# Two GNN layers on one core: mask loading reordered in the opening, and the search for negative mask values moved to later steps

## The chip, the cores and the metric

The kernel runs on one core of a Trainium2 chip. The metric is device time in microseconds. TensorE (PE in the profile) multiplies matrices into PSUM; VectorE (DVE), ScalarE (ACT) and GpSimd (POOL) work on tiles in SBUF, the first two also on PSUM; SyncE (SP) issues most DMAs. Each engine works through its own queue in program order.

## The reference

The input x is (8, 2048, 256) in float32, adj is a (2048, 2048) int32 mask with 0 and 1. Two layers follow each other, each added to its input:

```python
h = jnp.maximum(_layernorm(x, axis=-1), 0.0)
x = x + _L0_gnn_ref(h, adj, ...)   # 4 heads of 64; softmax inside each chunk of 256 keys
h = jnp.maximum(_layernorm(x, axis=-1), 0.0)
x = x + _L1_gnn_ref(h, adj, W, a)  # e = leaky(e_src + e_dst), masked, softmax over 2048 keys, elu
```

In the first layer the mask enters as

```python
scores = jnp.clip(scores, -10.0, 10.0)
mask = adj_matrix.reshape(N, Nc, CHUNK)[None, None]
scores = jnp.where(mask == 0, jnp.asarray(-10.0, scores.dtype), scores)
attn = jax.nn.softmax(scores, axis=-1)
ctx = jnp.einsum('bhnjc,bhjcd->bhnd', attn, vc)
```

and in the second as `mask = adj > 0`. The two tests agree unless adj holds a negative value. So the kernel looks for negative values, and if there is one (or if one of three other bounds is broken) a slower second version of the second layer runs behind the fast one.

## The kernel before

**Masks.** The mask is used turned over, keys on partitions, as an fp8 tile `limit` of 128 x 4 x 16 x 512: -0.5 where a key is masked, +0.5 where it is not. A score tile is cut with one VectorE instruction, the minimum of the score and its limit (L537). `limits()` makes it from 32 parts of 128 query rows by 1024 keys. For each part: `fetch` (SP loads 512 KB of int32, L262), `turn_over` (ScalarE casts it to bf16, L268, and SP issues a transposing DMA, L272), `find_negative` (ScalarE takes relu(-mask) with a sum over the row into `below`, L283; for the first four parts VectorE takes a minimum, L280 and L281), and `compare` (VectorE writes `limit`, L287). Two raw buffers alternate, so the load of part k + 2 waits for cast and search of part k. One `next` of `mask_turns` does `turn_over`, `find_negative` and the next `fetch`; one of `mask_compares` does one `compare`.

**The order before the loop** is written out by hand: loads of x, Wk, Wq, two biases, two mask parts, the next block of x, Wv, Wo, three bias rows and bv; then the transposes of Wk and Wq; then a string of letters, each one step of a generator: b the first batch's work (normalised rows h, their transposes hT, projections to K and Q), r the statistics of x, m a mask turn, c a compare; then the transposes of Wv and Wo, one compare, two mask turns and one b.

**The main loop** (from `for n in range(-2, len(steps))`) has 256 steps: 8 batches, 4 blocks of 512 queries, 4 chunk pairs by 2 head pairs. Step n makes the scores of step n + 2 (S, 4 tiles of 128 x 1024: TensorE L529, VectorE L537), takes their exponentials (E, ScalarE L543), weighs V with the tiles of step n (C, L551) and adds up the sums of step n + 1 (A, L564). ScalarE copies the sums from PSUM (L575), a DMA regroups them (`sum<-s`), VectorE inverts them (L582), a DMA writes them out (`inv<-sum`) and two read them back spread over the partitions (`r<-inv`), and VectorE scales by them (L603, L605). In mid-step (M, between E2 and C1) and at its end stands `mask_part()`: one compare and one mask turn each, so all 32 parts are done by step 11.

Other work is put between: `tick()` runs the generators in `quiet` (loads, statistics, and the end of a query block, `finish`: where n % 8 is 1 ScalarE makes four rows o from x, L650), and `advance()` those in `aside` (normalised rows L153, transposes L171, projections L162 with PSUM copies L378 for K and Q and L357 for V, the output projection). Scores, projections and sums share three PSUM pairs under the tag "big". The h tiles have a ring of three buffers.

After the loop the second layer runs over 32 passes of 16 key tiles, and the test of `below` comes at the end of it.

Of the kernel before, what the change touches and what calls it, by code (L numbers as in the profile page):

```python
# [10 lines left out]
I32 = mybir.dt.int32  # L11
FP8 = mybir.dt.float8e5
AF = mybir.ActivationFunctionType
ALU = mybir.AluOpType
PSUM = bass.MemoryType.PSUM

P = 128
# [34 lines left out]
def layers(  # L52
# [18 lines left out]
    nc = tc.nc  # L71
# [8 lines left out]
    NT = QB // P  # L80
# [3 lines left out]
    big = ctx.enter_context(tc.tile_pool(name="big", bufs=2))  # L84
    small = ctx.enter_context(tc.tile_pool(name="small", bufs=2))
# [16 lines left out]
    def aux(dtype=F32):  # L102

        return rest[0] if rest else pair(dtype)[:, 0, :]
# [26 lines left out]
    power = const.tile([P, 1], F32, tag="power", name="power")  # L131
# [70 lines left out]
    quiet = []  # L202
# [8 lines left out]
    def tick():  # L211
        moved = False
        for steps_of in list(quiet):
            got = next(steps_of, quiet)
            if got is quiet:
                quiet.remove(steps_of)
            moved = moved or got is not False
        return moved
# [13 lines left out]
    def drain(until=lambda: False):  # L232
        while not until() and advance():
            pass


    limit = const.tile([P, NQB, NKT, QB], FP8, tag="limit", name="limit")
    below = const.tile([P, NQB, 2 * NT], F32, tag="below", name="below")
# [6 lines left out]
    adj_in = [big.tile([P, 1024], I32, tag="kv", name="adj_in", bufs=12) for _ in range(2)]  # L245
    masks = big.tile([P, 2, 1024], BF16, tag="kv", name="masks", bufs=12)
    two_turned = big.tile([P, 2, 8, P], BF16, tag="c1", name="turned", bufs=1)
    turned_masks = [two_turned[:, 0], two_turned[:, 1], big.tile([P, 8, P], BF16, tag="r", name="turned", bufs=1)]
# [5 lines left out]
    def limits():  # L254

        parts = [(qb, t, half) for qb in range(NQB) for half in range(2) for t in range(NT)]

        def fetch(k):
            qb, t, half = parts[k]
            q0 = qb * QB + t * P  # L260
            raw = adj_in[k % 2]
            nc.sync.dma_start(raw, adj[q0 : q0 + P, half * 1024 : (half + 1) * 1024])  # L262
            return raw

        def turn_over(k):

            m = masks[:, k % 2]
            nc.scalar.copy(  # L268
                m.rearrange("p (b t c r) -> p b c t r", b=2, t=NT, c=2),
                raws[k].rearrange("p (b c t r) -> p b c t r", b=2, c=2, t=NT),  # L270
            )
            nc.sync.dma_start(turned_masks[k % 3], m, transpose=True)  # L272

        def find_negative(k):

            qb, t, half = parts[k]
            found = below[:, qb, 2 * t + half : 2 * t + half + 1]
            if k < NT:
                least_of = small.tile([P, 1], I32, tag="bad", name="lowest", bufs=1)
                nc.vector.tensor_reduce(least_of, raws[k], mybir.AxisListType.X, ALU.min)  # L280
                nc.vector.tensor_scalar(found, least_of, 0.0, -1.0, ALU.min, ALU.mult)  # L281
            else:
                nc.scalar.activation(raws[k], raws[k], AF.Relu, scale=-1.0, accum_out=found)  # L283

        def compare(k):
            qb, t, half = parts[k]
            nc.vector.tensor_scalar(  # L287
                limit[:, qb, half * 8 : (half + 1) * 8, t * P : (t + 1) * P],
                turned_masks[k % 3], 0.0, 0.5, ALU.not_equal, ALU.subtract, saturate=False,
            )  # L290
            if t == NT - 1:
                made.append((qb, half))

        raws = [fetch(k) for k in range(2)]

        def turns():
            for k in range(len(parts)):
                turn_over(k)
                find_negative(k)
                if k + 2 < len(parts):  # L300
                    raws.append(fetch(k + 2))
                yield

        def compares():
            for k in range(len(parts)):
                compare(k)
                yield

        return turns(), compares()

    qkv, norm_of = {}, {}

# [143 lines left out]
    first_batch = batch(0)  # L456
    next(first_batch)
    next(quiet[0])
    PART = {"q": 0.5 / EDGE, "k": 1.0}
    wT, raw_of = {}, {}  # L460

    def fetch_weights(name, w, tag):

        raw_of[name] = big.tile([P, FC, F], F32, tag=tag, name="w_raw", bufs=2)
        nc.sync.dma_start(raw_of[name], w.rearrange("(c p) f -> p c f", p=P))

    def turn_weights(name):

        wT[name] = const.tile([P, FC, F], F32, tag=f"w{name}", name=f"w{name}")
        for ic in range(FC):  # L470
            ps = aux()[:, :F]
            for oc in range(FC):
                nc.tensor.transpose(
                    ps[:, oc * P : (oc + 1) * P], raw_of[name][:, oc, ic * P : (ic + 1) * P], ident
                )
            nc.scalar.copy(wT[name][:, ic, :], ps)
# [3 lines left out]
    bcol = {}  # L480
# [2 lines left out]
        nc.sync.dma_start(bcol[name], v.rearrange("(c p) -> p c", p=P))  # L483
    mask_turns, mask_compares = limits()
    next(quiet[0])
    fetch_weights("v", Wv, "o")
    fetch_weights("o", Wo, "o")
    brow = {}
    for name, v in (("o", bo), ("gamma", gamma), ("beta", beta)):
        brow[name] = const.tile([P, F], F32, tag=f"r{name}", name=f"r{name}")  # L490
# [1 line left out]
    bv_col = small.tile([P, 2], F32, tag="bv", name="bv", bufs=1)  # L492
    nc.sync.dma_start(bv_col, bv.rearrange("(s p) -> p s", p=P))

    turn_weights("k")
    turn_weights("q")
    nc.scalar.mul(bcol["q"], bcol["q"], PART["q"])
    for what in "b b m b b m m c b b m c r b b c".split():
        next({"b": first_batch, "r": quiet[0], "m": mask_turns, "c": mask_compares}[what])
    turn_weights("v")  # L500
    turn_weights("o")
    for what in (mask_compares, mask_turns, mask_turns, first_batch):
# [2 lines left out]
    def bias():  # L505
        spread_bv = big.tile([P, 2, P], F32, tag="h", name="spread_bv", bufs=3)
        nc.vector.tensor_copy(spread_bv, bcast(bv_col, 2, P))
        yield from later()
        ps = aux()[:, :F]
        for s in range(2):  # L510
            nc.tensor.matmul(
                ps, spread_bv[:, s, :], wT["o"][:, s, :], start=(s == 0), stop=(s == 1)
            )
        nc.vector.scalar_tensor_tensor(brow["o"], ps, float(NCH), brow["o"], ALU.mult, ALU.add)
        yield
# [376 lines left out]
    def last_batch():  # L892
        yield from batch(B - 1)
        aside.append(sources_of(W, a))
        yield from preparation(0)
# [30 lines left out]
    weights, totals, r = {}, {}, None  # L926
    ORDER = [(kind, int(t)) for kind, t in "S0 E0 S1 E1 C0 S2 E2 M0 C1 S3 E3 C2 C3 B0 A0".split()]
    for n in range(-2, len(steps)):
        here[0] = n
        if n >= 0:  # L930
            b, qb, c = steps[n]
            blk, hp = divmod(c, 2)
            if n == NT:
                aside.append(bias())
            b1 = 1 if n == 1 else b + 2 if (qb, c) == (NQB - 1, NCH - 2) else B
            if b1 < B:
                aside.append(batch(b1) if b1 + 1 < B else last_batch())
            if b == B - 1 and c == NCH - 2 and qb < NQB - 1:
                aside.append(fill(qb))
            drain(lambda: len(qkv[b][2]) > blk)  # L940
            both = banks("both")
            v = qkv[b][2][blk]
        coming = prepared(steps[n + 2]) if n + 2 < len(steps) else iter(())
        inside = -1 <= n < len(steps) - 1
        weights[n + 2] = []
        for kind, t in ORDER:
            if kind in "SE":
                weights[n + 2] += [e for e in (next(coming, None),) if e is not None]
            elif kind == "A":
                if inside:  # L950
                    sums = pair()[:, 0, :256]
                    add_up(totals.pop(n + 1), sums)
                    got = divide(sums)
            elif kind == "B":
                if 0 <= n < 4:
                    advance(False)
            elif kind == "M":
                mask_part()
            elif n >= 0:
                weigh(hp, t, weights[n][t], v, both)  # L960
        weights.pop(n, None)
        if n + 2 < len(steps):
            totals[n + 2] = added(weights[n + 2])
        if n >= 0:
            if c == 0:
                accs[qb] = heads_tile("acc", "acc")
            accumulate(accs[qb][:, hp, :], both, r, blk == 0)
            if c == NCH - 1:
                finish(b, qb, accs[qb])
        held = invert(got) if inside else None  # L970
        if n >= 0:
            tick()
        if inside:
            r = spread(held)
        fetch_all()
        for _ in range({-2: 5, 3: 2}.get(n, 3 if n < NQB * NCH else 2)):
            advance(n < 0)
        mask_part()
# [55 lines left out]
    bad = small.tile([P, 4], F32, tag="bad", name="bad", bufs=1)  # L1034
# [148 lines left out]
    for s, (k, jt) in enumerate(rounds):  # L1183
        here[0] = len(steps) + s // 4
        at[0] = s
        b, h = passes[k]
# [19 lines left out]
        m = jt // 2  # L1206
# [320 lines left out]
```

## Time and profile before

| | us |
|---|---|
| median of 3 runs (lowest to highest) | 3971.54 (3970.2 to 3981.95) |
| profiled execution | 3974.03 |
| its span | 3972.2 |

| stretch, us | PE busy | ACT busy | DVE busy | DMA share | GB/s |
|---|---|---|---|---|---|
| 0 to 210 | 170.96 | 159.47 | 136.70 | 0.75 | 174 |
| 210 to 420 | 202.45 | 121.77 | 168.35 | 0.28 | 75 |
| 300 to 2600 | 2256.16 | 1395.90 | 1923.93 | 0.32 | 85 |

The first 210 us hold all the mask work. Instructions that the change touches: the cast L268 32 x 1.03 us, the search L283 28 x 1.06 us with an accumulator read of 0.19 each, the search L280 4 x 1.22 us, the compare L287 32 x 0.68 us (median), the transposing DMA L272 32 issues of 1.26 us (median) on SP.

In such lines a bracket gives the engine's idle time ahead of the instruction and what ended it; "SPq" is SP issuing a DMA, whose length there is that of the issue, not of the transfer. In the lines of digits each digit is the busy share of a slice in tenths.

### The profile page before, as it was taken

How to read it: one execution, taken by the hardware profiler on the slowest of the kernel's cores; microseconds unless marked ns; L12 is line 12 of the kernel's file. 1: busy time of each engine (PE TensorE's matmuls, PEld its weight loads, DVE VectorE, ACT ScalarE, POOL GpSimd, SP SyncE). 2: the span in 40 equal slices, each digit the busy share in tenths (PEclk: the TensorE clock that was granted, in tenths of full speed). 3: DMA queues.
4: the chain of work that ended last, by engine and by line, in shares of the span. 5: the costliest groups of instructions: out<-in, count | busy, mean ns of one | idle time of the engine just before them, and what ended most of it. 6: DMA issues, size and time to landing. Idle time of an engine off the chain costs nothing.

```text
span 3972.2 us, 93255 instructions
## 1 busy us (share of the span) xinstructions
PE 3846.7 (97%) x38454; PEld 1359.6 (34%) x38454; DVE 3409.6 (86%) x3920; ACT 2527.0 (64%) x3635; POOL 3380.8 (85%) x1763
## 2 busy tenths in 40 slices
PE   7899999999999999999999998989999999999997
PEld 2233333333333333333333333323333333333332
DVE  5778888888888888888888877879999999999998
ACT  7756556666566566656665656556766667676666
POOL 4678899999899899999999988858778778788887
PEclk9999999999999999999999999999999999999999
DMA  7723333333333333333333333322223122232222
GB/s 184 175 74 82 82 82 88 82 83 93 83 82 85 84 84 82 90 84 80 86 90 81 77 91 84 88 75 78 57 66 76 47 74 67 55 72 62 55 55 50
DMA packets 379442, 324.33 MB, mean 82 GB/s; under 512 B 261504, under 2 KB 329856, under 8 KB 379008
## 3 DMA queue, kind: packets, MB, share of 16 engines
q1 hardware_dynamic: 373312, 301.24, 29.8%
q0 software_dynamic: 4608, 16.78, 1.2%
q8 instruction: 304, 4.98, 0.5%
q14 instruction: 130, 1.06, 0.1%
q10 hardware_dynamic: 1088, 0.26, 0.0%
HBM read 271.26 MB, written 36.18 MB: 77 GB/s over the span
## 4 chain that ended last, share of the span: by engine, by line
PE 64%; DMA 13%; DVE 9%; POOL 5%; ACT 4%; issue 3%; SPq 1%; DVEq 0%; POOLq 0%; ACTq 0%
PE acc L1003 17%; PE big L529 15%; PE both L551 13%; PE big L162 7%; PE den L1014 6%; DMA r<-inv 5%; POOL t L1214 3%; DMA sum<-s 3%; DMA inv<-sum 3%; DVE E L537 3%; PE rest L162 2%; PE big L564 2%; DVE e L993 2%; ACT E L543 2%; DMA x<-in_x_dram 2%
## 5 line engine op out<-in xcount | busy, mean ns | idle before, releaser
L543 ACT ACTIVATE E<-E 128x1024 f32<-128x1024 f32 x1024 | 1081.8, 1058 | 683.1 <-DVE E L537 623.8
L537 DVE SCALAR_TENSOR_TENSOR E<-big,limit 128x1024 f32<-128x1024 f32 x1024 | 1198.6, 1214 | 91.5 <-PE big L529 85.9
L923 POOL TENSOR_TENSOR add<-add,E 128x1024 f32<-128x1024 f32 x512 | 1216.3, 2376 | 40.3 <-ACT E L543 0.2
L993 DVE SCALAR_TENSOR_TENSOR e<-near,far,limit 128x2048 f32<-128x2048 f32 x512 | 1166.6, 2341 | 30.7 <-issue 16.1
L529 PE MATMUL big<-qT,kT 64*64 64x512 f32 x8192 | 1069.6, 601 | 34.7 <-DVE E L537 11.8
L551 PE MATMUL both<-E,v 64*64 64x512 f32 x8192 | 1075.1, 592 | 9.4 <-DVE acc L605 6.2
L1214 POOL TENSOR_TENSOR t<-t,e 128x1024 f32<-128x1024 f32 x384 | 911.7, 2420 | 188.3 <-PE den L1014 99.7
L1003 PE MATMUL acc<-e,qn 128*32 128x512 f32 x8192 | 979.1, 595 | 11.8 <-DVE e L993 11.6
L921 POOL TENSOR_TENSOR add<-E 128x1024 f32<-128x1024 f32 x256 | 629.2, 2458 | 209.1 <-ACT E L543 208.7
L1173 ACT ACTIVATE t<-e,quot 128x1024 f32<-128x1024 f32 x384 | 419.8, 1141 | 200.3 <-PE den L1014 148.8
L551 PEld LDWEIGHTS both<-E,v 64*64 64x64 f32 x8192 | 341.8, 134 | 588.0 <-issue 502.1
L529 PEld LDWEIGHTS big<-qT,kT 64*64 64x64 f32 x8192 | 293.6, 133 | 613.0 <-issue 342.8
L1003 PEld LDWEIGHTS acc<-e,qn 128*32 128x32 f32 x8192 | 270.6, 110 | 554.9 <-issue 467.6
L603 DVE TENSOR_TENSOR both<-both,r 128x512 f32<-128x512 f32 x448 | 310.8, 694 | 165.1 <-DMA r<-inv 118.9
L605 DVE TENSOR_TENSOR acc<-both,acc 128x512 f32<-128x512 f32 x448 | 309.8, 692 | 15.3
L1014 PE MATMUL den<-t,for_sums 128*32 128x512 f32 x1536 | 230.6, 593 | 7.7 <-POOL t L1214 7.6
L564 PE MATMUL big<-add,both_of 128*32 128x256 f32 x2048 | 164.0, 392 | 0.0
L1014 PE MATMUL den<-e,for_sums 128*32 128x512 f32 x1024 | 149.9, 592 | 0.0
L582 DVE RECIPROCAL sum<-sum 128x16 f32<-128x16 f32 x256 | 63.7, 249 | 87.8 <-DMA sum<-s 83.8
L162 PE MATMUL big<-hT,wk 128*32 128x512 f32 x1024 | 125.1, 610 | 9.9 <-ACT hT L179 9.9
L1131 ACT ACTIVATE z<-z,dens 128x64 f32<-128x64 f32 x496 | 124.6, 334 | 2.0 <-DVE z L1115 2.0
L162 PE MATMUL big<-wv,hT 128*32 128x256 f32 x2048 | 123.5, 383 | 1.4 <-ACT hT L179 1.3
(142 smaller groups left out, 3060.7 us busy)
## 6 DMA issues: line engine op xcount, KB each, us to landing
r<-inv SPq DMA_DIRECT2D x512, 256.0 KB
x<-in_x_dram SPq DMA_DIRECT2D x96, 512.0 KB
es<-er SPq DMA_DIRECT2D x64, 512.0 KB
adj_in<-in_adj_dram SPq DMA_DIRECT2D x32, 512.0 KB
x<-o POOLq DMA_DIRECT2D x32, 512.0 KB, 4.4
x<-x SPq DMA_DIRECT2D x32, 512.0 KB
xh<-x SPq DMA_DIRECT2D x128, 128.0 KB
out_dram<-xh SPq DMA_DIRECT2D x124, 128.0 KB
```

The costliest lines, as they stand in the source:

```text
L162: nc.tensor.matmul(to[32 * j : 32 * j + 32], lhsT[:, n : n + 32], rhs, start=start, stop=stop)
L529: nc.tensor.matmul(ps[64 * c : 64 * c + 64, hh, :], ks[blk][own, hp, keys : keys + 64], qs[qb][own, hp, :], start=True, stop=True,)
L537: nc.vector.scalar_tensor_tensor(e, ps, -0.5, bcast(limit[:, qb, NT * blk + t, :], 1, 2), ALU.max, ALU.min)
L543: nc.scalar.activation(e, e, AF.Exp, scale=0.25 * EDGE)
L551: nc.tensor.matmul(both[c][64 * hh : 64 * hh + 64, :], v[own, t, mine], e[own, hh, :], start=(t == 0), stop=(t == NT - 1),)
L921: nc.gpsimd.tensor_tensor(total, tiles[0], tiles[1], ALU.add)
L923: nc.gpsimd.tensor_tensor(total, total, e, ALU.add)
L993: nc.vector.scalar_tensor_tensor(e, near, far[:, jt, h : h + 1], limit[:, :, jt, :], ALU.max, ALU.min)
L1003: nc.tensor.matmul(acc[part][32 * blk : 32 * blk + 32, :], qn[jt // NT][:, jt % NT, own], e[:, blk, :], start=(jt == 0), stop=(jt == NKT - 1),
L1014: nc.tensor.matmul(den[32 * blk : 32 * blk + 32, :], for_sums[:, jt, :], blocks[blk], start=first, stop=last,)
L1173: nc.scalar.activation(t, e[:, 2 * half : 2 * half + 2, :], AF.Copy, scale=shared[b][4][:, jt // 2, h : h + 1],)
L1214: nc.gpsimd.tensor_tensor(ts[half], ts[half], now[:, 2 * half : 2 * half + 2, :], ALU.add)
```

## The change

- Four raw parts are loaded at once: parts 2 and 3 into the two buffers of the tag "add", which the loop's sums use later. Parts 4 and 5 are fetched after the casts of parts 0 and 1, so a load follows the cast by four parts there and by two afterwards.
- The casts stand between the steps of the first batch (the new string of letters). The loads of Wv and Wo come after the first two mask turns, the bias rows and bv after the whole string; the transposes of Wk and Wq come first.
- `find_negative` leaves the mask turn. It now reads `limit`, two key tiles by 512 queries at a time (1024 fp8 values a partition), into an fp8 tile of the h ring, and runs on ScalarE once in every step with n % 4 = 1 from 33 to 157, 32 in all, after `tick()` and ahead of the `r<-inv` loads and `advance()`.
- `compare` takes the minimum of the mask and 1, less 0.5, instead of a test against 0, less 0.5. A negative mask value then gives a limit below -0.5.

```diff
--- before.py
+++ after.py
@@ -258,7 +258,7 @@
         def fetch(k):
             qb, t, half = parts[k]
             q0 = qb * QB + t * P
-            raw = adj_in[k % 2]
+            raw = big.tile([P, 1024], I32, tag="add", name="adj_in") if k in (2, 3) else adj_in[k % 2]
             nc.sync.dma_start(raw, adj[q0 : q0 + P, half * 1024 : (half + 1) * 1024])
             return raw
 
@@ -271,34 +271,23 @@
             )
             nc.sync.dma_start(turned_masks[k % 3], m, transpose=True)
 
-        def find_negative(k):
-
-            qb, t, half = parts[k]
-            found = below[:, qb, 2 * t + half : 2 * t + half + 1]
-            if k < NT:
-                least_of = small.tile([P, 1], I32, tag="bad", name="lowest", bufs=1)
-                nc.vector.tensor_reduce(least_of, raws[k], mybir.AxisListType.X, ALU.min)
-                nc.vector.tensor_scalar(found, least_of, 0.0, -1.0, ALU.min, ALU.mult)
-            else:
-                nc.scalar.activation(raws[k], raws[k], AF.Relu, scale=-1.0, accum_out=found)
-
         def compare(k):
             qb, t, half = parts[k]
             nc.vector.tensor_scalar(
                 limit[:, qb, half * 8 : (half + 1) * 8, t * P : (t + 1) * P],
-                turned_masks[k % 3], 0.0, 0.5, ALU.not_equal, ALU.subtract, saturate=False,
+                turned_masks[k % 3], 1.0, 0.5, ALU.min, ALU.subtract, saturate=False,
             )
             if t == NT - 1:
                 made.append((qb, half))
 
-        raws = [fetch(k) for k in range(2)]
+        raws = [fetch(k) for k in range(4)]
 
         def turns():
             for k in range(len(parts)):
                 turn_over(k)
-                find_negative(k)
-                if k + 2 < len(parts):
-                    raws.append(fetch(k + 2))
+                coming = k + 4 if k < 2 else k + 2
+                if k not in (2, 3) and coming < len(parts):
+                    raws.append(fetch(coming))
                 yield
 
         def compares():
@@ -307,6 +296,16 @@
                 yield
 
         return turns(), compares()
+
+    def find_negative(k):
+
+        qb, half, t = k // 8, k % 8 // NT, k % NT
+        room = big.tile([P, 1024], FP8, tag="h", name="room", bufs=3)
+        nc.scalar.activation(
+            room.rearrange("p (k q) -> p k q", k=2),
+            limit[:, qb, 8 * half + 2 * t : 8 * half + 2 * t + 2, :],
+            AF.Relu, scale=-1.0, bias=power[:, 0:1], accum_out=below[:, qb, 2 * t + half : 2 * t + half + 1], saturate=False,
+        )
 
     qkv, norm_of = {}, {}
 
@@ -483,8 +482,17 @@
         nc.sync.dma_start(bcol[name], v.rearrange("(c p) -> p c", p=P))
     mask_turns, mask_compares = limits()
     next(quiet[0])
+    turn_weights("k")
+    turn_weights("q")
+    nc.scalar.mul(bcol["q"], bcol["q"], PART["q"])
+    def begin(letters):
+        for what in letters.split():
+            next({"b": first_batch, "r": quiet[0], "m": mask_turns, "c": mask_compares}[what])
+
+    begin("m b m b b")
     fetch_weights("v", Wv, "o")
     fetch_weights("o", Wo, "o")
+    begin("m b c m b c b r b b c")
     brow = {}
     for name, v in (("o", bo), ("gamma", gamma), ("beta", beta)):
         brow[name] = const.tile([P, F], F32, tag=f"r{name}", name=f"r{name}")
@@ -492,11 +500,6 @@
     bv_col = small.tile([P, 2], F32, tag="bv", name="bv", bufs=1)
     nc.sync.dma_start(bv_col, bv.rearrange("(s p) -> p s", p=P))
 
-    turn_weights("k")
-    turn_weights("q")
-    nc.scalar.mul(bcol["q"], bcol["q"], PART["q"])
-    for what in "b b m b b m m c b b m c r b b c".split():
-        next({"b": first_batch, "r": quiet[0], "m": mask_turns, "c": mask_compares}[what])
     turn_weights("v")
     turn_weights("o")
     for what in (mask_compares, mask_turns, mask_turns, first_batch):
@@ -970,6 +973,8 @@
         held = invert(got) if inside else None
         if n >= 0:
             tick()
+        if n >= 33 and n % 4 == 1 and n // 4 - 8 < 32:
+            find_negative(n // 4 - 8)
         if inside:
             r = spread(held)
         fetch_all()
```

## The prediction

> **What bounds the kernel now.** I read the page first, then the chain of waits, the timeline, and the DMA load in quarter microseconds.
>
> ```profile
> span 3972.2 us, 93255 instructions
> PE 3846.7 (97%) x38454; PEld 1359.6 (34%) x38454; DVE 3409.6 (86%) x3920; ACT 2527.0 (64%) x3635; POOL 3380.8 (85%) x1763
> ...
> PE   7899999999999999999999998989999999999997
> ...
> DMA  7723333333333333333333333322223122232222
> ```
>
> TensorE is full except in the first slices, which are the ones where DMA is full. The stretches say the same: TensorE 171.0 of the first 210 us, 2256 of the 2300 us from 300 to 2600. So there are two places where this change can act: the opening, up to step 11 (about 205 us), where masks are made, and the 32 steps that get the search. Whatever either gives or takes stays to the end, since TensorE has nothing to catch up with.
>
> In the opening the chain of waits puts 28 searches (L283) on the path at about 1.15 us each ("130.35 0.94 issue" and "131.29 0.19 ACT adj_in L283" are the inside of one). The timeline of one step shows what else is there:
>
> ```profile
> 129.26 1.03 ACT L268 CAST masks<-adj_in 128x1024 bf16<-128x1024 int32 x1
> ...
> 130.32 1.23 SPq L272 DMA_TRANSPOSE turned<-masks  x1
> 130.32 1.06 ACT L283 ACTIVATE adj_in<-adj_in 128x1024 int32<-128x1024 int32 x1
> ...
> 131.64 0.53 SPq L262 DMA_DIRECT2D adj_in<-in_adj_dram  x1
> ...
> 132.33 0.35 ACT L575 COPY s<-big 128x256 f32<-128x256 f32 x1
> ...
> 132.71 0.67 SPq L577 DMA_DIRECT2D sum<-s  x1
> ...
> 135.83 0.25 DVE L582 RECIPROCAL sum<-sum 128x16 f32<-128x16 f32 x1 [3.17 <-DMA sum<-s]
> ```
>
> Times are start and length. The cast ends, SP issues the transpose for 1.23 us and at once the next mask part. Beside that, ScalarE searches, does the last exponential and copies the sums. The sums leave at 132.71 and land only 3.1 us later; after step 11, without masks, they need 1.8 to 2.1. The DMA load from 128 us on, a digit per 0.25 us, says why:
>
> ```profile
> DMA  9998799799964189964998869975200000012000
> ```
>
> It is busy until 135.25: the sums land when transpose and mask part have drained.
>
> The later place is a step with n % 8 = 1, here n = 49:
>
> ```profile
> 591.58 0.37 ACT L575 COPY s<-big 128x256 f32<-128x256 f32 x1
> 594.29 2.08 ACT L650 ACTIVATE o<-x,off,rstd 128x256 f32<-128x256 f32 x4 [2.34 <-DMA x<-in_x_dram]
> 596.27 0.67 ACT L378 ACTIVATE qT<-big,bq 128x512 f32<-128x512 f32 x1
> ...
> 596.99 1.09 PE L529 MATMUL big<-qT,kT 64*64 64x512 f32 x8 [1.01 <-ACT qT L378]
> ```
>
> ScalarE waits for x, does four o rows, then empties the PSUM pair of qT; TensorE has already stopped for that pair. Where n % 8 = 5 it is the other way round, ScalarE waits for TensorE:
>
> ```profile
> 477.44 0.69 ACT L378 ACTIVATE kT<-big,bk 128x512 f32<-128x512 f32 x1 [1.05 <-PE big L162]
> ```
>
> **Part one, the loads and the order before the loop.** Parts 2 and 3 go out behind 0 and 1 (two issues of 0.5 us, so x's second block leaves at 5.3 us, not 4.3; its first reader ran at 23.7, so this costs nothing). Wv, Wo, three bias rows and bv (0.51 + 0.68 + 0.92 + 0.34 + 0.43 + 0.38 us of SP's time) go behind the first transposes. Part 0 lands at 9.5 (VectorE's search, L280, waited for it until 9.58). ScalarE now casts it ahead of the first h, which started at 8.98: cast to 10.6, two h to 11.7, cast to 12.7, hT copy to 13.3, two h to 14.4, cast to 15.4, hT copy to 16.0. So K's first matmul moves from 14.79 to 16.05, **1.3 us later**. K and Q took until 24.2 and now take until 25.4; the copies of wv and wo end at 27.4 (26.1). From there it is faster. Parts 4 and 5 are in (issued at about 10.7 and 14 behind the transposes; before, part 5 came at 29.0), and two searches are gone: casts to 29.5, two h to 30.5, then the three E exponentials, which started at 32.2, **1.7 us earlier**. The next cast ends at 34.75 (36.1), then its transpose, mask part 8, and x's last block at 36.7 instead of 38.11. Its landing at 43.14 is what the chain waits for: **-1.4 us**. Bounds: DMA was idle 2.5 us before that landing (29.75 to 31, 36 to 37.25) and the bytes ahead of it are the same, so no more than -2.5; if the late K stays, +1.3. VectorE's four searches (1.22 + 0.15 us each) are hidden by its wait for data; the compare with a minimum costs what the compare with not-equal did, 0.68 us, since only the operation differs.
>
> **Part two, steps -1 to 11, 26 searches gone.** The one at a step's end lies in the wait for the sums: nothing, but for steps 2 and 3 where it delayed an exponential (0.4 by TensorE's idle time there, and 0.3). The one in mid-step delays the last exponential and the sums by 1.06 us (start to next start). But without it the sums cannot leave before SP has issued transpose and part, 1.23 + 0.1 + 0.53 + 0.1 = 1.96 us after the cast; now it is 2.4. That leaves 0.4, and the drain takes most of that: in steps 6, 7 and 8 the sums were there 3.73, 3.79 and 3.83 us after the mask part's issue, whenever they left. Transpose and part themselves leave no sooner. I take nothing for steps 4 to 9, 0.5 and 0.6 for steps 0 and 1, where the sums left late behind an hT copy, and 0.7 for step 10, which fetches no part: **-2.5 us** in all. Bounds: 0, and 13 x 1.06 = -13.8 if the sums followed their own issue.
>
> The Trainium skill (DMA: Bandwidth & Descriptors, section Queues, rings and completion order) says that a DMA's semaphore increment lands only after every earlier write of that DMA engine. By that rule the sums cannot overtake the mask part and steps 4 to 9 give nothing; by a fixed latency from their own issue they would give 0.4 each, 2.4 us more. The load row above agrees with the rule for one step.
>
> **Part three, 32 searches in steps 33 to 157.** The nearest rows are fp8 to fp8 at the same size:
>
> ```profile
> L882 ACT ACTIVATE limit<-limit x32: 1039/1046/1062, 2351.1 to 2640.7; 128x1024 fp8e5<-128x1024 fp8e5 x32
> ```
>
> and L283 with its accumulator read, after which the next instruction starts 1.06 us after the search did. I take 1.06; 1.25 if the read did not overlap. The search follows the o rows and goes ahead of the PSUM copies on ScalarE's queue.
> - 16 steps with n % 8 = 5: ScalarE sat idle 1.05 to 1.4 us before the kT copy. The search fills this: 0 (at most 0.2 each, 3.2).
> - 16 steps with n % 8 = 1: I read, for each, the end of the qT or v copy and the start of the third group of score matmuls. In 12 (41, 49, 57, 65, 97, 105, 113, 121, 129, 137, 145, 153) at most 0.07 us lay between: 12 x 1.01 = 12.1. In 73, 81, 89 it was 0.63, 0.92, 0.66: 0.43 + 0.14 + 0.40 = 1.0. In 33 it was 1.25: 0. Sum **+13.1 us**.
> The queue behind the search holds that copy and the next step's exponentials, which had up to 1.9 us of room; TensorE waits for the copy. From 400 to 1640 us TensorE's listed waits are only 10.4 us, 5.5 of them for just these copies, so little is left to absorb a stall. Lower bound 0, if x landed a microsecond earlier, as it does in step 33; upper 16 x 1.25 + 3.2 = 23. The search's output takes a slot of the h ring (three), whose last readers, the transposes at n % 8 = 3 and 4, are done; limit is written again only from 2351 us. No wait from these.
>
> **Sum.** -1.4 - 2.5 + 13.1 = +9.2 us. The profiled run took 3974.0 (span 3972.2 and 1.8 around it), so 3983.2; it is 2.5 above the median of 3971.5, on which the forecast is **3980.7**, its own range 3975 to 3987.
>
> **Rivals.**
> 1. *The sums follow their own issue*, so every mid-step search was on the path: -13.8 - 1.4 + 13.1 = -2, 3969. For it: the chain of waits counts the search. Against: landing times tied to the part's issue.
> 2. *Faster*: the same, and the later searches fall into ScalarE's idle time (36% over the span), x landing earlier: -15 to -16, 3956. Against: ScalarE is idle there because it waits in order, ahead of the search, not behind it.
> 3. *Slower*: the opening gives nothing, because the cold, late K chain (+1.3) stays ahead of the exponentials, and each late search costs 1.25 at n % 8 = 1 and 0.1 at 5: 1.3 + 15.6 + 1.6 = +18.5, 3990. It decides if K's first matmul comes after 16 us and the first exponential after 32.2.
> 4. *Half the late price*: where x lands varies with DMA traffic that the change shifts; if 6 of the 12 tight steps become like step 33, the late part is 6.6 and the net +2.7: 3974. For it: the copy's room runs from 0 to 1.25 us in the same kind of step.
>
> **Chances.** Forecast 0.53, rival 1 0.10, rival 2 0.13, rival 3 0.15, rival 4 0.09. What a measurement of this kernel can tell from no change is about 0.3%, 11.9 us: below 3959.6 or above 3983.5. The forecast's own range crosses the upper bound: 0.24 of its 0.53 lies above. Faster: 0.13 and a little of rival 1, 0.15. Slower: 0.24 + 0.15 = 0.39. Same: 0.46. The range, 3963 to 3989, leaves out most of rival 2 and half of rival 3.
>
> **What would show it.** Right: the first exponential of E near 30.5 us and x's last block landing near 41.7; in steps 4 to 9 sums that leave 0.4 us earlier and land no earlier; the search between the o rows and the qT or v copy, and TensorE's waits for those copies at n % 8 = 1 grown from 5.5 to about 18 us; nothing at n % 8 = 5. Wrong: steps 5 to 9 shorter by a microsecond each, or no growth of the waits for qT and v.

## The result, and the profile after

Over 18 runs each the changed kernel has a median of 3981.98 us (3973.18 to 3990.58), the kernel before 3973.66 (3963.61 to 3981.95). The ratio is **1.0022**, with a 95% interval of 1.0015 to 1.0029: 8 to 9 us slower, inside the 0.3% taken as no change, but clear of 1. In a later group of runs it was 1.0028 (1.0019 to 1.0038). Forecast: 3980.7, +9.2.

The page of the changed kernel, the lines that answer to those of before:

```profile
span 3982.2 us, 93224 instructions
PE 3842.7 (96%) x38454; PEld 1398.1 (35%) x38454; DVE 3404.5 (85%) x3912; ACT 2530.4 (64%) x3643; POOL 3375.1 (85%) x1763
...
DMA  7722333333333333332332332322223222222222
```

TensorE does the same work in a span 10 us longer. Step 49 of the changed kernel in the timeline (start, length, engine; in brackets the idle time ahead and what ended it):

```profile
592.30 0.37 ACT L578 COPY s<-big 128x256 f32<-128x256 f32 x1
...
594.49 2.07 ACT L653 ACTIVATE o<-x,off,rstd 128x256 f32<-128x256 f32 x4 [1.81 <-DMA x<-in_x_dram]
596.47 1.13 ACT L304 ACTIVATE room<-limit,power 128x1024 fp8e5<-128x1024 fp8e5 x1
597.50 0.18 ACT L304 ACTIVATION_READ_ACCUMULATOR room<-limit,power 128x1 f32 x1
597.60 0.67 ACT L377 ACTIVATE qT<-big,bq 128x512 f32<-128x512 f32 x1
...
598.32 1.09 PE L532 MATMUL big<-qT,kT 64*64 64x512 f32 x8 [1.68 <-ACT qT L377]
```

The search stands between the o rows and the qT copy, and TensorE waits 1.68 us for that copy; before it was 1.01. The list of waits of TensorE from 400 to 1640 us (total, times, longest), first the kernel before, then the changed one:

```profile
PE big L529 <- ACT qT L378: 4.6, 7, 1.0
...
PE big L529 <- ACT v L357: 0.9, 2, 0.5
```

```profile
PE big L532 <- ACT qT L377: 14.8, 11, 2.1
PE big L532 <- ACT v L356: 3.3, 3, 1.9
```

5.5 us have become 18.1. Where n % 8 is 5, here n = 37, the search only fills the wait: the kT copy starts 1.41 us after the copy of the sums (477.64 to 479.05), as it did before (476.03 to 477.44).

```profile
477.64 0.35 ACT L578 COPY s<-big 128x256 f32<-128x256 f32 x1
477.89 1.15 ACT L304 ACTIVATE room<-limit,power 128x1024 fp8e5<-128x1024 fp8e5 x1
...
479.05 0.69 ACT L377 ACTIVATE kT<-big,bk 128x512 f32<-128x512 f32 x1
```

The opening did not go as forecast. ScalarE's timeline there, in the changed kernel:

```profile
12.34 1.09 ACT L153 ACTIVATE h<-x,off,rstd 128x256 f32<-128x256 f32 x2
15.51 1.04 ACT L268 CAST masks<-adj_in 128x1024 bf16<-128x1024 int32 x1 [2.08 <-DMA turned<-masks]
16.46 0.58 ACT L179 COPY hT<-big 128x512 f32<-128x512 f32 x1
17.93 1.04 ACT L268 CAST masks<-adj_in 128x1024 bf16<-128x1024 int32 x1 [0.89 <-DMA turned<-masks]
...
31.36 2.94 ACT L546 ACTIVATE E<-E 128x1024 f32<-128x1024 f32 x3
```

The third cast waits 2.08 us for the transposing DMA of the first part to land, and the fourth 0.89 us for that of the second: the buffer of the cast masks has two halves only, and each is free again once its transpose has read it. K's first matmul comes at 17.09 (before 14.79, forecast 16.05), the first exponential at 31.4 (32.2, forecast 30.5), x's last block lands at 43.95 (43.14, forecast 41.7).

### The profile page after: what moved, and what is told of

The parts are those of the page before. It is cut to its first block, busy times and chain, and to the rows that moved or that the text cites. A ratio compares the mean times of both kernels' runs of the same rounds, so it can differ in the third digit from the quotient of the medians.

```text
span 3982.2 us, 93224 instructions
## 1 busy us (share of the span) xinstructions
PE 3842.7 (96%) x38454; PEld 1398.1 (35%) x38454; DVE 3404.5 (85%) x3912; ACT 2530.4 (64%) x3643; POOL 3375.1 (85%) x1763
## 3 DMA queue, kind: packets, MB, share of 16 engines
q14 instruction: 130, 1.06, 0.1%
## 4 chain that ended last, share of the span: by engine, by line
PE 66%; DMA 13%; DVE 7%; POOL 5%; ACT 4%; issue 3%; SPq 1%; DVEq 0%; POOLq 0%; ACTq 0%
PE acc L1008 18%; PE big L532 15%; PE both L554 14%; PE big L162 7%; PE den L1019 6%; DMA r<-inv 4%; POOL t L1219 3%; DMA sum<-s 3%; DMA inv<-sum 2%; DMA x<-in_x_dram 2%; PE rest L162 2%; PE big L567 2%; DVE E L540 2%; DVE e L998 1%; DVE both L606 1%
## 5 line engine op out<-in xcount | busy, mean ns | idle before, releaser
L1008 PEld LDWEIGHTS acc<-e,qn 128*32 128x32 f32 x8192 | 297.1, 110 | 530.1 <-issue 401.7
```

Source lines behind the costliest of these rows:

```text
L1008: nc.tensor.matmul(acc[part][32 * blk : 32 * blk + 32, :], qn[jt // NT][:, jt % NT, own], e[:, blk, :], start=(jt == 0), stop=(jt == NKT - 1),
```

## The experiments

Each ratio is to the kernel before on the same chip, with its 95% interval. The chips differ by up to 0.5% in absolute time, so only ratios are compared across groups; within a group, medians.

**No late search.** Edit of the changed kernel:

```diff
+    nc.vector.memset(below, 0.0)
-        if n >= 33 and n % 4 == 1 and n // 4 - 8 < 32:
-            find_negative(n // 4 - 8)
```

> The changed kernel without its 32 searches (the search for negative values is left out; below is set to 0). Theory A, the late searches cost some 12 us and the new opening gives nothing: 3972 to 3976, within 0.1% of the kernel before; its step 32 is as late as in the changed kernel. Theory B, the new opening is what costs 8 us: 3980 to 3984, unchanged. Theory C, the forecast's sum, opening -3.9 and late +13.1: 3969 to 3970.

Measured 0.9988 (0.9978 to 0.9997), 3964.24 us. The opening alone is no loss; theory B falls. In total it is theory C, the forecast's -3.9: 0.12% of 3968 is 4.8 us, and the medians are 4.2 apart. Theory A's gain of nothing lies outside the interval, but only just. TensorE's waits for the copies are 3.7 and 0.8 us.

**No search in the opening of the kernel before.**

```diff
-                find_negative(k)
+    nc.vector.memset(below, 0.0)
```

> The kernel before with its 32 searches in the opening left out (below is set to 0), all else as it was. If a search in mid-step was on the path with its full 1.06 us, 13 of them and the two between the casts before the loop give 14 to 16 us: 3958 to 3960. If the sums land with the drain of the transpose and the mask part behind which they are queued, whenever they leave, 2 to 5 us: 3969 to 3972, and the sums leave about 0.4 us earlier in steps 5 to 9 and land no earlier.

Measured 0.9994 (0.9981 to 1.0007), 3965.96 us: 2.5 us by the medians and not clear of 0, but nothing like 14 us. In steps 6, 7 and 8 the sums left 0.67, 0.83 and 0.66 us after the mask part's issue (1.05, 1.06 and 1.06 before) and were there 3.84, 3.99 and 3.68 us after it (3.73, 3.79 and 3.83). They left earlier and landed no earlier.

**Only the searches at n % 8 = 5, and only those at 1.**

```diff
-        if n >= 33 and n % 4 == 1 and n // 4 - 8 < 32:
+        if n >= 33 and n % 8 == 5 and n // 4 - 8 < 32:
```

and with `n % 8 == 1` in the other run.

> The changed kernel with only the 16 searches of steps with n % 8 = 5 (the other 16 mask parts are not searched). Theory A, a search costs what it adds to the wait for the PSUM copy behind it: the same as without any search, within 2 us. Rival, a search costs by ScalarE's load wherever it stands, 0.35 us each: 5 to 6 us above the kernel without searches, half way to the changed kernel.

> The changed kernel with only the 16 searches of steps with n % 8 = 1 (the other 16 mask parts are not searched). Theory A: the whole late cost, 10 to 13 us above the kernel without searches, like the changed kernel, and TensorE's waits for the qT and v copies between 400 and 1640 us near 18 us. Rival, cost by load: 5 to 6 us above the kernel without searches.

Same chip, same group as the run without any: 3963.19 us (0.9985, 0.9975 to 0.9995) with those at 5, 3979.29 (1.0027, 1.0015 to 1.0039) with those at 1, 3964.24 with none. So 16 searches cost nothing that shows in one place and 15.0 us in the other, on the same engine and of the same length, and the intervals of the two ratios lie apart. ScalarE's load is not the cost: by the rival each set of 16 would have cost 5 to 6 us. TensorE's waits in the run with those at 1:

```profile
PE big L533 <- ACT qT L378: 14.2, 11, 2.2
PE big L533 <- ACT v L357: 3.4, 3, 1.7
```

17.6 us, against 4.5 without searches: 13.1 of the 15 are in these two rows.

**All 32 at n % 8 of 5 and 6.**

```diff
+        if n >= 37 and n % 8 in (5, 6) and n < 160:
+            find_negative(2 * (n // 8 - 4) + n % 8 - 5)
```

> The changed kernel with all 32 searches, one in each step with n % 8 of 5 and 6 between 37 and 158. Theory A, only a search ahead of a late PSUM copy costs: as without any search, 0.9980 to 0.9996 of the kernel before. Rival, step 6 of the eight is no better than step 1: 1.001 to 1.003.

Measured 0.9993 (0.9983 to 1.0004), 3951.22 us: the whole search at no cost that shows; the rival's 1.001 lies outside the interval.

**The search ahead of tick().**

```diff
+        if n >= 33 and n % 4 == 1 and n // 4 - 8 < 32:
+            find_negative(n // 4 - 8)
         if n >= 0:
             tick()
-        if n >= 33 and n % 4 == 1 and n // 4 - 8 < 32:
-            find_negative(n // 4 - 8)
```

> The changed kernel with the search emitted ahead of tick(), so that at n % 8 = 1 it stands on ScalarE between the copy of the sums and the o rows, where ScalarE waits for x. Theory A: the wait for x, 0.2 to 3.2 us, takes it in; the five or six steps with a wait under 1.06 us lose 0.3 to 0.9 each, 2 to 4 us in all: 0.9985 to 1.0005 of the kernel before. Rival, the place within the step does not matter: 1.002 to 1.003, as the changed kernel.

Measured 0.9987 (0.9977 to 0.9997), 3952.10 us. A move by one call recovers the loss. ScalarE in step 49 of this run, and the third group of score matmuls on TensorE:

```profile
587.69 1.15 ACT L304 ACTIVATE room<-limit,power 128x1024 fp8e5<-128x1024 fp8e5 x1
588.74 0.19 ACT L304 ACTIVATION_READ_ACCUMULATOR room<-limit,power 128x1 f32 x1
590.45 2.07 ACT L653 ACTIVATE o<-x,off,rstd 128x256 f32<-128x256 f32 x4 [1.52 <-DMA x<-in_x_dram]
592.43 0.67 ACT L377 ACTIVATE qT<-big,bq 128x512 f32<-128x512 f32 x1
...
593.15 1.09 PE L532 MATMUL big<-qT,kT 64*64 64x512 f32 x8 [0.74 <-ACT qT L377]
```

The same instruction, now ahead of the wait for x, which takes it in. TensorE still waits for the qT copy, but 0.74 us instead of 1.68; over the same stretch its waits for the copies are 2.7 and 0.7 us.

**Four cast buffers.** On top of the searches at 5 and 6:

```diff
+            if k == 2:
+                more.append(big.tile([P, 2, 1024], BF16, tag="acc", name="masks"))
-            m = masks[:, k % 2]
+            m = (more[0] if k in (2, 3) else masks)[:, k % 2]
```

> As the run with the searches at 5 and 6, and four cast buffers for the first four parts instead of two, so that the casts of parts 2 and 3 need not wait for the transposing DMAs of parts 0 and 1. If these two waits (2.1 and 0.9 us in the changed kernel) hold the opening back: casts 2 and 3 near 13.4 and 15 us, K's first matmul near 15.5 instead of 17.1, step 32 some 1.5 us earlier. If the DMA queue holds it back, since the transposes drain in order behind the loads: the casts are earlier, E's first exponential and step 32 are not, within 0.7 us.

Measured 0.9987 (0.9977 to 0.9996), 3951.23 us, level with 3951.22. The cause of the late casts is confirmed:

```profile
13.26 1.03 ACT L270 CAST masks<-adj_in 128x1024 bf16<-128x1024 int32 x1
14.20 0.58 ACT L179 COPY hT<-big 128x512 f32<-128x512 f32 x1
14.67 1.04 ACT L270 CAST masks<-adj_in 128x1024 bf16<-128x1024 int32 x1
...
28.29 2.94 ACT L548 ACTIVATE E<-E 128x1024 f32<-128x1024 f32 x3
```

Both waits are gone. Against the run with two buffers K's first matmul comes at 14.82 us (16.79), the first exponential at 28.3 (30.4), and x's last block lands at 41.0 (42.9). But the sums of step -1 leave at 51.2 us (53.0 with two buffers), those of step 0 at 65.5 (65.2), those of step 32 at 425.1 (426.0). The lead is gone in one step, so neither expectation holds whole: casts and exponential follow the first, the time the second. In the chain of waits the end of step 0 is now TensorE's own work (0.59 us of transposes, 0.57 of adding up and 3.71 of projections, back to back).

**The old opening without its searches, all 32 at 5 and 6.** On the kernel before: the searches of the opening are left out as in the second experiment, the new search stands where the fifth has it, and the compare is the changed one.

> The opening of the kernel before without its searches (compare with the minimum, as in the change), and all 32 searches at n % 8 of 5 and 6. If the searches there cost nothing: as the kernel before without searches, 0.998 to 1.0005. If the new opening has a worth of its own beyond the searches taken out, it is 1 to 3 us above the run with the changed opening and the same searches; if not, level with it.

Measured 0.9983 (0.9974 to 0.9992), 3949.95 us, level with 3951.22 for the changed opening and the same searches. This one beats both kernels: 0.17% below before, some 0.4% below the change.

**Both kernels again, on one chip.** No edit.

> The kernel before once more, for a trace from the same chip as the next two: 1.000 of itself, and step 32 within 1.5 us of the other two.

> The changed kernel once more: 1.0015 to 1.0029 of the kernel before. If the new opening is worth 3 to 4 us, its step 32 comes that much ahead of the kernel before on this chip; if what the runs without late searches gained comes in the later steps, step 32 is level within 1.5 us.

The kernel before: 0.9998 (0.9989 to 1.0007). The changed one: 1.0028 (1.0019 to 1.0038), 3966.67 us; its waits for the copies are 14.3 and 4.8 us. The sums of step 32 leave at 425.6 us before and at 429.2 after: here the opening is 3.6 us behind, where ahead or level was expected. Eight traces with this opening gave 424.6 to 429.2, so a single trace can't tell what it is worth.

**Two searches in each step with n % 8 = 1.**

```diff
+        if n >= 33 and n % 8 == 1 and n // 8 - 4 < 16:
+            for two in range(2):
+                find_negative(2 * (n // 8 - 4) + two)
```

> The changed kernel with all 32 searches in the 16 steps with n % 8 = 1, two in each, none at 5. Theory A, each search there delays a copy TensorE waits for, by 1.06 us: two cost 2.1 in the 12 tight steps, 1.2 to 1.5 in the three with some room, 0.9 in step 33, about 30 us above no search and 16 to 18 above the changed kernel: 1.0055 to 1.0075 of the kernel before. Rival, a search costs by ScalarE's load wherever it stands: as the changed kernel, 1.002.

Measured 1.0014 (1.0005 to 1.0024), 3960.33 us. Theory A's 1.0055 to 1.0075 fails. The rival's 1.002 lies in the interval, but not its reason, "as the changed kernel": that took 3966.67 us on the same chip, 6.3 more, so twice the work at the bad place costs less. TensorE's waits say that it is not the same place any more:

```profile
PE big L532 <- DVE E L540: 11.2, 17, 1.2
PE big L532 <- DVE o L639: 2.3, 4, 0.7
PE big L532 <- ACT v L356: 0.6, 1, 0.6
PE big L532 <- ACT qT L377: 0.4, 1, 0.4
```

The third score group no longer waits for the qT copy but for VectorE to empty the first group: in step 49 it starts at 594.21 us, ahead of the copy at 595.41. The built programs show why. These are the PSUM banks of the pairs from the sums of step 48 on, in program order (A sums, q projection, S scores):

```
changed kernel, n = 49:   A 0   q 2   S 4   S 0   S 2   S 4
two searches,   n = 49:   A 4   q 0   S 2   S 4   S 2   S 0
```

With one search the third group takes the bank of the projection, with two it takes that of the first group, and the projection's bank goes to the fourth. The tag "big" gives out its three buffers in an order that can change with the instructions around; it is not a fixed turn. In the kernel before and in all other runs here the order of sums, projections and scores in the main loop is that of the changed kernel, so those runs differ in where the search stands and not in the banks. So the kernel with two searches isn't twice the changed one, and theory A holds only with its condition: a search in front of a PSUM copy costs what it adds to that copy where the next group waits for that bank.

## Why the prediction was right

The number was right: the large term by its mechanism, the two small ones by luck.

**The bound.** TensorE's waits outside the opening are a few microseconds, so each stall went to the end. Right.

**Late searches, +13.1.** Right in its mechanism and near in its size. Shown by the runs with those at 5 and at 1: 0 (-1.05 us between the medians) and 15.0 us. The search holds the next instruction back 1.13 us (596.47 to 597.60), not 1.06, which was taken from the int32 search; with 1.13 the same list of 16 steps gives 12 x 1.08 + 0.50 + 0.21 + 0.47 = 14.1. The forecast of 18 us of waits met 18.1, but as a sum and not step by step, since x lands at other times in each trace: in step 121 ScalarE waited 1.88 us for x before and 0.35 after, and TensorE 0.49 us for the copy before and none after, while in step 137 TensorE's wait went from 0.16 to 1.74.

**Mask steps, -2.5.** The claim that the sums land with the mask part was right for the three steps it was read from. The Trainium skill's rule (DMA: Bandwidth & Descriptors, section Queues, rings and completion order), that an increment lands after every earlier write of its DMA engine, agrees with the run without searches: 0.2 to 0.4 us less between part and sums, and 3.7 to 4.0 us from part to landing, about as before. The step that fails is steps 0 and 1, for which 0.5 and 0.6 us were taken: the sums of step 0 leave 12.4 us after those of step -1 and 12.8 us ahead of those of step 1 in the changed kernel, 12.2 and 12.7 before. Nor does the whole stretch show 2.5 us: from the sums of step -1 to those of step 11 it takes 151.7 and 153.7 us in the two traces of the kernel before, 152.7 in that kernel without searches and 155.1 in the changed one.

**Opening, -1.4.** This term was wrong in its working. Of the order "two h to 14.4, cast to 15.4" the cast began only at 15.5, because it waits for a half of the mask buffer. The forecast counted data and queues and left out that buffer: a load issued earlier brings its cast no further than the next buffer behind it. So K's projection was 2.3 us late instead of 1.3; mask part 6 left at 30.8, the cast that needs it ran at 35.6 instead of 33.7, and x's last block came 0.8 us later, not 1.4 earlier. The path was wrong too: with four cast buffers that block landed 1.9 us earlier than with two, and nothing of it was left at step 0.

**And yet the two together.** With late searches absent or harmless, the new opening measures 0.9988, 0.9985, 0.9993, 0.9987 and 0.9987, the old one without searches 0.9994 and 0.9983. Both come to a mean near 0.9988, though single intervals reach from 0.9974 to 1.0007: by this estimate some 4.6 us come from taking 32 searches out of the opening, and none that can be told from the new order of loads and casts (in like pairs the changed opening is 1.7 us faster than the old one and 1.3 slower). With the 15.0 of the late searches that makes +10.4, against 8.3 and 10.7 measured. The forecast had -3.9 for the opening, by terms of which one was wrong and the other does not show in the traces: that the size came out right is luck. Where along the span the 4.6 us arise stays open: the sums of step 32 leave at 426.4 and 425.6 us in the two traces of before, at 424.6 to 426.7 in the runs counted here.

**The rivals.** That every mid-step search was on the path fell with the second experiment. That the late ones are hidden is true at 5 and 6 and ahead of tick(), not where the change puts half of them. That the K chain stays ahead of the exponentials did not happen in the first trace: K's first matmul came after 16 us, as that rival had it, but the exponentials came 0.8 us earlier in spite of it (level, 31.97 and 32.01 us, in the later pair). That half of the late price goes away with the landing of x did not happen: the waits are 18.1 and 19.1 us in the two traces of the changed kernel.

## What to carry to other kernels

An engine's idle time is not one pool: the same 1.13 us was free in one step of eight and cost a microsecond in another, and what decides is whether the instruction stands behind or ahead of the wait that makes the idle time, and whether a PSUM copy that the bounding engine needs is queued behind it. When a load is moved forward, follow it through each buffer down to its last consumer; the first buffer not enlarged takes the wait over. A chain of waits names the instruction that came last, which is not the same as what would come last without it: look for the second one (here SP's issue and the drain of the DMA queue, behind a search that the chain shows with 1.15 us in each step) before counting its whole length as a gain.

## What the runs showed of the hardware that had not been expected

An fp8 ACTIVATE of 128 x 1024 with bias and row sum took 1.14 us and its read of the sum 0.19; in step 49 the next instruction started 1.13 us after it. The same size without bias and sum took 1.05, and the int32 one with a sum and no bias 1.06. In the opening of the changed kernel, with the DMA engines busy throughout, issuing one transposing DMA held SP for 3.26 us (19.00 to 22.26) and another for 2.40 (12.13 to 14.53), against a median of 1.26 before; the loads behind them on SP waited as long. That the full queue is the cause is not shown: another issue at 16.58, with DMA as busy, took 1.23.
